# First mixture of a perceiver block: three dense tiles and five tiles by expert blocks, changed to eight tiles by expert blocks in two groups

## The chip, the cores and the metric

The kernel runs on one core of one Trainium2 chip. The metric is the device time of one launch in microseconds. All data are float32.

## The reference, cut to what matters

x is 16 x 64 x 256 (1024 tokens of width 256), the context is 16 x 1601 x 256. Six residual stages follow each other, each on the normalised x:

```
x = x + deformable_attention(ctx, ctx, norm(x))   # 16 heads, 5 sampled keys per query and head
x = x + sigmoid_attention(norm(x))                # inside a batch of 64 tokens
x = x + mixture0(norm(x))                         # 8 experts, hidden width 512, top 2
x = x + cross_attention(norm(x), ctx)             # 16 heads of 64; 77 text and 1524 image keys
x = x + state_space(norm(x))                      # scan over 64 tokens
x = x + mixture1(norm(x))                         # 32 experts, hidden width 128, top 4

def mixture0(x):
    p = softmax(router(rms(x)));  w = top-2 of p, renormalised, times per_expert_scale
    y_e = (gelu(x @ gate_e.T) * (x @ up_e.T)) @ linear_e
    return sum_e w_e * y_e
```

A token needs only two of the eight experts. The choice is made by the data, so a kernel can either run all experts on all tokens of a tile and weight the results (dense), or sort tokens by expert into blocks of 128 rows and run one expert per block.

## The kernel before, in words

The 1024 tokens lie in `x4` as 8 tiles of 128 tokens (two batches of 64 each). Work on TensorE, VectorE and ScalarE is issued in the order in which the Python generators are advanced (`tc.manual_schedule`); SyncE (SP) issues weight and context loads, GpSimd (POOL) issues the indirect DMAs, each engine in its own program order.

*Keys and values.* `keys_values` runs in 113 steps: it turns pieces of the context (`cx` to `cxt`), multiplies them by `wkv` (TensorE, L381) and ScalarE copies the result to `kv` (L382), which goes to the tables `tab` in DRAM (L385). Beside it run `samples` (where each head looks), `texts` (until step 60) and, from step 60 on, what stands in the list `mids`.

*Gathers and attends.* There are 32 units (8 tiles by 4 groups of 4 heads). `gather` does half a unit: VectorE copies the indices (`ig`, L427), then POOL issues ten indirect DMAs (L429). `attend` is the VectorE and ScalarE work of a unit (L449 to L481), in two halves. Their place in the program is chosen by `tick`, a count of microseconds that is only an estimate made while the program is built: a gather no sooner than `APART` (16) after the one before, `APART_X` (12) from the cross-attention on; an attend no sooner than `AFTER` (42) after its gather was issued.

*Attention and first mixture (middle).* `attention` finishes the deformable attention of one or two tiles and does the sigmoid attention. `middle` does the router. For tiles 0 to 2 (`ND0 = 3`) it goes on to run all eight experts on the whole tile (dense), two tiles as one group and one tile alone, each expert as two gate loads and one linear load of 512 KB into the four buffers `w`. For tiles 3 to 7 it writes the normalised rows to `x0d` and the routing to a `Table`; `slots` sorts, and `gelus` runs 17 blocks of 128 rows: an indirect DMA fetches the rows (`xb`, L853), SP reads the expert's number and loads 1.5 MB of its weights into five buffers `w`, and the result goes to `y0d`. `combine` fetches each token's two results back (`yk`, L654) and adds them to x.

*Cross-attention.* `Cross.step` is called 131 times; each does one pair of heads of one batch. TensorE multiplies the folded query `qf` with the turned context (`st`, shown at L88, the helper `mm`), VectorE takes maxima (`mp`, L1090), the maximum is turned and spread (L1109, `mc` L1121), VectorE subtracts and ScalarE exponentiates (L1130, L1131), and TensorE multiplies by the context (L1059) one step later. `fold(n + 1)` (L1123) makes the query of the next pair. Two batches make a tile, so 16 steps use one tile of x; they can go no further than the tiles whose first mixture is done. A step takes up to four generators (`side`, `mid`, `more`, `late`), which it advances at four places.

*The order at the top.* Keys and values with the first tiles beside them; the rest of those tiles alone; cross steps 0 to 26 with the remaining gathers and attends; cross steps 27 to 41 with attention and first mixture of tiles 3 to 7, what is left of it being drained before step 42; cross steps 42 to 130 with the state space of three quarters of the tokens; then the second mixture.

```python
        side = chain([middle(ND0, 1, lp, mw, tb0)]
                     + [z for t0 in range(ND0 + 1, NPAIR, TG) for z in (attention(t0, TG, lp, mw), middle(t0, TG, lp, mw, tb0))]
                     + [tb0.slots, lambda: gelus(lp, tb0), lambda: combine(lp, tb0, ND0, y0d, lambda t: None, 1)])
        while side.gi_frame and cr.n < NHP * 2 * ND0 - 6:
            cr.step(side, side, side, side)
            next(side, None)
        drain(side)
```

Of the kernel before, what the change touches and what calls it, by code (L numbers as in the profile page):

```python
# [27 lines left out]
APART, APART_X, AFTER = 16.0, 12.0, 42.0  # L28
# [25 lines left out]
ND0 = 3  # L54
# [11 lines left out]
def perceiver_kernel(ctx: ExitStack, tc: tile.TileContext, a: dict, out: bass.AP):  # L66
# [369 lines left out]
    def attend(i):  # L436

        j, h0 = units[i]
        if j not in cvs:
            cvs[j] = mk(const, [P, D], "cv", bufs=NPAIR - ND0)  # L440
# [101 lines left out]

    NT0 = NPAIR - ND0
    x0d, y0d = mk(dram, [NT0 * P, D], "x0d"), mk(dram, [blocks_of(NT0, E0, TOP0) * P, D], "y0d")
# [125 lines left out]
    class Middle:  # L670

        def __init__(self, lp, tag=None):
            self.tag = "x" if tag else "z"

            def wload(name, n, src):
                return load(lp, tag or name, src, [P, KC, n], 5 if tag else 1)

            self.bs = biases(lp, "lbias", ("bo", "abqkv", "abo", "als", "pes"), a["bias_a"])
            qkv = a["awqkvT"].rearrange(kp, p=P)
            self.wo = wload("wo", D, a["woT"].rearrange(kp, p=P))  # L680
            self.wqkv = [wload("wqk", 2 * D, qkv[:, :, : 2 * D]), wload("wv", D, qkv[:, :, 2 * D :])]
            self.awo = wload("awo", D, a["awoT"].rearrange(kp, p=P))

    def attention(t0, nt, lp, mw):
# [16 lines left out]
        xn = normed(range(t0, t0 + nt), mw.tag, lp)  # L701
# [3 lines left out]
        xt = turned(xn, nt, mw.tag, lp)  # L705
# [50 lines left out]
    def middle(t0, nt, lp, mw, tb=None):  # L756


        tiles = range(t0, t0 + nt)
        tok = nt * P  # L760
        xg = x4[:, t0 : t0 + nt, :]

        def wload(src, shape):
            return load(lp, "w", src, shape, 4)

        xn = normed(tiles, "x", lp)
        if tb is not None:
            q0 = (t0 - ND0) * P
            nc.sync.dma_start(out=x0d[q0 : q0 + tok, :].rearrange("(t p) d -> p t d", p=P), in_=xn)
        yield  # L770


# [9 lines left out]
        cw = mk(lp, [P, nt, E0], "cw")  # L782
        for t in range(nt):
# [6 lines left out]
            c = cw[:, t, :]  # L790
            if tb is not None:
                j = tiles[t] - ND0
                c = tb.gate[:, j, :]
                nc.vector.tensor_copy(tb.mask[:, j, :], m)
                tb.number(j)
# [9 lines left out]
        if tb is not None:  # L805
            return
        nh = HID0 // 2
        held = None

        def second(e, act, lin):  # L810
            po = bank()[:, : nt * D].rearrange("p (t d) -> p t d", t=nt)
            for t in range(nt):
                mm(po[:, t, :], [(act[:, c, t * P : (t + 1) * P], lin[:, c, :]) for c in range(HID0 // P)])
                nc.vector.scalar_tensor_tensor(
                    xg[:, t, :], po[:, t, :], cw[:, t, e : e + 1], xg[:, t, :], ALU.mult, ALU.add
                )

        for e in range(E0):
            act = mk(lp, [P, HID0 // P, tok], "act")
            lin = None  # L820
            for hf in range(2):
                wg = wload(a["gate0"][e, hf].rearrange("(k p) i h -> p k i h", p=P), [P, KC, 2, nh])
                if hf:
                    lin = wload(a["lin0"][e].rearrange("(c p) d -> p c d", p=P), [P, HID0 // P, D])
                for c in range(nh // P):
                    ph = bank()[:, : 2 * tok].rearrange("p (i n) -> p i n", i=2)
                    for i in range(2):
                        mm(ph[:, i, :], [(wg[:, k, i, c * P : (c + 1) * P], xt[:, k, :]) for k in range(KC)])
                    if held and hf * 2 + c == 1:
                        second(*held)  # L830
                        held = None
                    gl = mk(lp, [P, tok], "gl")
                    nc.scalar.activation(gl, ph[:, 0, :], AF.Gelu_apprx_tanh)
                    nc.vector.tensor_tensor(act[:, hf * 2 + c, :], gl, ph[:, 1, :], ALU.mult)
                    yield
            held = (e, act, lin)
        second(*held)
        yield

    def gelus(lp, tb):  # L840
# [4 lines left out]
        def fetch(i):  # L845
            if i >= tb.nb:
                return
            if i % 4 == 0:
# [5 lines left out]
                out=x, out_offset=None, in_=x0d, in_offset=bass.IndirectOffsetOnAxis(ap=tb.row[:, i : i + 1], axis=0)  # L854
# [3 lines left out]
            for hf in range(2):  # L858
                w.append(load(lp, "w", a["gate0"][bass.ds(v, 1), hf].rearrange("o (k p) i h -> p (o k) i h", p=P), [P, KC, 2, nh], 5))
            w.append(load(lp, "w", a["lin0"][bass.ds(v, 1)].rearrange("o (c p) d -> p (o c) d", p=P), [P, HID0 // P, D], 5))  # L860
# [10 lines left out]
        def second(i, act, lin):  # L871
            po = bank()
            mm(po[:, :D], [(act[:, c, :], lin[:, c, :]) for c in range(HID0 // P)])
            y = mk(lp, [P, D], "y")
            nc.scalar.copy(y, po[:, :D])
            nc.scalar.dma_start(out=y0d[i * P : (i + 1) * P, :], in_=y)
# [30 lines left out]
    class Cross:  # L907
# [98 lines left out]
        def fold(self, n):  # L1006
# [10 lines left out]
            qf = self.qf[n] = mk(self.xp, [P, KC, P], "qf", bufs=2)  # L1017
# [52 lines left out]
        def step(self, side=None, mid=None, more=None, late=None):  # L1070
# [52 lines left out]
            self.fold(n + 1)  # L1123
# [43 lines left out]
        def begin(self, xp):  # L1167
# [16 lines left out]
            self.fold(0)  # L1184
            yield
# [6 lines left out]
    class Ssm:  # L1192
# [15 lines left out]
        def group(self, g, wide=None):  # L1208
# [67 lines left out]
            dx = mk(mp, sh, "dx")  # L1276
# [466 lines left out]
```

## Time and profile before

| what | value |
|---|---|
| median of 3 runs | 3313.22 us (3308.72 to 3315.46) |
| the profiled execution | 3307.06 us, its span 3305.1 us |
| busy: TensorE, VectorE, ScalarE, GpSimd | 2924.7, 1620.0, 1026.4, 818.2 us |
| granted TensorE clock, mean | 0.946 |
| moved by DMA | 326.06 MB, 99 GB/s over the span |

The span is read by stages, since the limits differ:

| stage | us from the span's start |
|---|---|
| keys and values, with two tiles' attention and 5 of 8 dense experts beside them | 0 to 711 |
| the remaining dense work, alone | 711 to 885 |
| the cross-attention's start | 885 to 912 |
| cross steps 0 to 26, with gathers and attends | 912 to 1402 |
| cross steps 27 to 41, with attention and mixture of tiles 3 to 7, and the drain | 1402 to 1811 |
| cross steps 42 to 130, with the state space | 1811 to 3005 |
| second mixture | 3005 to 3305 |

Busy times of TensorE are of matmul records, whose ends are modelled. Every float32 matmul leaves two records.

### The profile page before, as it was taken

The page shows a single profiled execution, that of the slowest core. Times are in us where ns is not written, and L with a number is a line of the kernel's source. Part 1 is how long each engine was busy: PE and PEld are TensorE (multiplying, and loading weights), DVE is VectorE, ACT ScalarE, POOL GpSimd, SP SyncE. Part 2 cuts the span into 40 slices and gives each one's busy share as a digit, 9 for nine tenths or more (in the row PEclk, how much of TensorE's full clock was granted, in tenths as well). Part 3 has the DMA queues.
Part 4 walks back from the last instruction along what each step waited for, and adds up shares of the span by engine and source line. Part 5 has one row for each costly group of instructions (what it writes and reads, how often), then busy time and mean ns, then how long its engine had stood idle before and what let it go on. Part 6 is the DMA issues. An engine that isn't in the chain of part 4 may idle for free.

```text
span 3305.1 us, 46546 instructions
## 1 busy us (share of the span) xinstructions
PE 2924.7 (88%) x17734; PEld 2402.8 (73%) x17734; DVE 1620.0 (49%) x4143; ACT 1026.4 (31%) x2379; POOL 818.2 (25%) x923
## 2 busy tenths in 40 slices
PE   8779887995678888987997999999999999998879
PEld 4444444564567777876897999989999999896667
DVE  2421113224345445655332577557654487655846
ACT  3233333323212211233242433334323333222421
POOL 0444335545455455200001011001100011000721
PEclk9889998997789899988998999999999999999999
DMA  6387754662511211200454121112210122003884
GB/s 203 102 148 159 239 155 128 180 194 83 154 24 30 58 52 38 75 23 30 137 175 148 44 62 59 50 45 71 66 34 30 57 66 63 26 1 115 257 239 123
DMA packets 339015, 326.06 MB, mean 99 GB/s; under 512 B 59349, under 2 KB 289017, under 8 KB 338281
## 3 DMA queue, kind: packets, MB, share of 16 engines
q1 hardware_dynamic: 186297, 225.11, 22.9%
q10 hardware_dynamic: 126928, 63.06, 7.0%
q0 software_dynamic: 25568, 34.91, 4.9%
q8 instruction: 141, 2.31, 0.3%
q14 instruction: 81, 0.66, 0.1%
HBM read 248.37 MB, written 74.62 MB: 98 GB/s over the span
## 4 chain that ended last, share of the span: by engine, by line
PE 74%; DVE 10%; another core or an unknown queue 5%; issue 4%; DMA 3%; ACT 3%; POOL 0%; SPq 0%; DVEq 0%; ACTq 0%; POOLq 0%
PE st L88 31%; PE mm L1059 19%; PE mm L88 15%; PE mm L153 5%; PE mm L1015 2%; DMA wg<-in_guT 1%; PE mm L1045 1%; DVE hs L1298 1%; DVE mp L1090 1%; PE mm L984 1%; DVE pt L1130 1%; DMA w<-in_gate 1%; PE mm L1109 1%; DVE hc L1303 0%
## 5 line engine op out<-in xcount | busy, mean ns | idle before, releaser
L88 PE MATMUL st<-qf,cT 128*128 128x128 f32 x6144 | 761.3, 282 | 42.2 <-ACT qf L1018 31.9
L429 POOL DMA_INDIRECT g<-tab,ig x640 | 616.2, 963 | 720.8 <-DVE ig L427 519.6
L88 PEld LDWEIGHTS st<-qf,cT 128*128 128x128 f32 x6144 | 739.8, 198 | 52.4 <-ACT qf L1018 35.6
L1059 PE MATMUL mm<-cn,pt 128*128 128x257 f32 (+1 forms) x3072 | 755.8, 390 | 2.0 <-DVE cT L84 1.2
L1059 PEld LDWEIGHTS mm<-cn,pt 128*128 128x128 f32 (+1 forms) x3072 | 563.8, 193 | 88.0 <-DVE cT L84 2.0
L88 PE MATMUL st<-wkv,cxt 128*128 128x512 f32 (+1 forms) x832 | 401.4, 629 | 53.7 <-ACT kv L382 28.7
L1090 DVE TENSOR_REDUCE mp<-st 128x128 f32<-128x512 f32 x384 | 261.1, 688 | 253.5 <-PE st L88 232.6
L88 PEld LDWEIGHTS st<-wkv,cxt 128*128 128x128 f32 (+1 forms) x832 | 157.0, 198 | 226.8 <-issue 178.1
L1130 DVE TENSOR_TENSOR pt<-st,mc 128x512 f32<-128x512 f32 (+1 forms) x384 | 224.2, 640 | 156.5 <-ACT mc L1121 133.9
L1131 ACT ACTIVATE pt<-pt 128x512 f32<-128x512 f32 (+1 forms) x384 | 207.3, 588 | 57.6 <-DVE pt L1130 51.2
L382 ACT COPY kv<-st 128x512 f32<-128x512 f32 (+1 forms) x208 | 118.9, 591 | 234.1 <-PE st L88 128.7
L1121 ACT COPY mc<-mm 128x128 f32<-128x128 f32 x128 | 33.9, 265 | 464.8 <-PE mm L1119 328.4
L1111 DVE TENSOR_REDUCE xmx<-mm 128x1 f32<-128x128 f32 x128 | 37.3, 292 | 229.3 <-PE mm L1109 180.1
L1068 ACT COPY ot<-mm 128x256 f32<-128x256 f32 x128 | 47.2, 369 | 294.8 <-PE mm L153 294.7
L920 POOL MEMSET cn<- 128x12 f32 x16 | 1.8, 119 | 544.5 <-PE mm L1059 520.3
L461 DVE TENSOR_REDUCE smx<-sc 128x4 f32<-128x20 f32 x32 | 5.4, 168 | 244.5 <-ACT sc L459 233.9
L1304 POOL TENSOR_TENSOR ys<-ys,hc 128x512 f32<-128x512 f32 x64 | 81.5, 1273 | 161.2 <-DVE hc L1303 160.9
L1388 POOL DMA_INDIRECT xb<-xnd,row x55 | 55.2, 1004 | 262.9 <-PE mm L1045 221.6
L88 PE MATMUL mm<-xt,w 128*128 128x256 f32 (+1 forms) x512 | 103.0, 359 | 14.3 <-issue 8.4
L88 PEld LDWEIGHTS mm<-xt,w 128*128 128x128 f32 x512 | 89.6, 218 | 31.0 <-issue 21.2
L1035 ACT COPY yt<-mm 128x64 f32<-128x64 f32 x128 | 27.2, 212 | 252.7 <-PE mm L88 230.6
L153 PEld LDWEIGHTS mm<-ident,cx 128*128 128x128 f32 (+1 forms) x416 | 54.9, 150 | 44.4 <-issue 31.7
(455 smaller groups left out, 3994.5 us busy)
## 6 DMA issues: line engine op xcount, KB each, us to landing
tab<-kv ACTq DMA_DIRECT2D x48, 1024.0 KB
w<-in_gate SPq DMA_DIRECT2D x66, 512.0 KB
cx<-in_ctx SPq DMA_DIRECT2D x48, 512.0 KB
cn<-in_ctx SPq DMA_DIRECT2D x16, 1408.0 KB
wg<-in_guT SPq DMA_DIRECT2D x87, 256.0 KB
w<-in_lin SPq DMA_DIRECT2D x33, 512.0 KB
wk<-in_xwkiT SPq DMA_DIRECT2D x32, 512.0 KB
wd<-in_down1T SPq DMA_DIRECT2D x87, 128.0 KB
```

The lines of the kernel that those rows point to most:

```text
L88: nc.tensor.matmul(o, lhsT=l, rhs=r, start=i == 0, stop=i == len(pairs) - 1)
L153: nc.tensor.transpose(t[:ncol, i, :rows], b, ident[:rows, :rows])
L382: nc.scalar.copy(kv[:w, :, c, :], pk[:w].rearrange("p (h e) -> p h e", h=H0))
L429: nc.gpsimd.indirect_dma_start(out=gf[:, (half * n + s) * 4 * HD0 : (half * n + s + 1) * 4 * HD0], out_offset=None, in_=tables[j], in_offs ...
L1015: nc.tensor.matmul(pf[:, k * P : (k + 1) * P], lhsT=w[:, hp % 4, k * P : (k + 1) * P], rhs=rhs, start=True, stop=True)
L1059: nc.tensor.matmul(po, lhsT=pt[:w, c, :], rhs=cn[:w, c, :], start=c == 0, stop=c == NCH - 1)
L1068: nc.scalar.copy(ot, tp[:, :KC, :])
L1090: nc.vector.tensor_reduce(mp_[:, i, :], s.rearrange("p c n -> p n c"), AX.X, ALU.max)
L1130: nc.vector.tensor_tensor(o, st[i][:, :m, :], mc.to_broadcast([P, m, P]), ALU.subtract)
L1131: nc.scalar.activation(o, o, AF.Exp)
L1304: nc.gpsimd.tensor_tensor(y, y, hc, ALU.add)
L1388: nc.gpsimd.indirect_dma_start(out=x, out_offset=None, in_=xnd, in_offset=bass.IndirectOffsetOnAxis(ap=tb.row[:, i : i + 1], axis=0))
```

## The change: what it does

All eight tiles take the way of blocks, in two groups of four tiles (`first(0)`, `first(1)`), 15 blocks each; the dense part is gone. The first group stands in `mids` beside keys and values, where `mid` is now called twice in a step; the second is the `side` of cross steps. Both use five buffers `w`, which also hold the attention's weights. The first group has tiles 2 and 3 attended singly, so that each can begin when its own units are done. `APART` is 12 everywhere. `fold` runs two pairs of heads ahead, with three buffers `qf`. In the state space `dx` and `ys` take the buffers of the tags `mt` and `mn`. `more` is given to every second step alone.

```diff
-APART, APART_X, AFTER = 16.0, 12.0, 42.0
+APART, AFTER = 12.0, 42.0
...
-ND0 = 3
+WB0 = 5
...
-            cvs[j] = mk(const, [P, D], "cv", bufs=NPAIR - ND0)
+            cvs[j] = mk(const, [P, D], "cv", bufs=4)
...
-    NT0 = NPAIR - ND0
-    x0d, y0d = mk(dram, [NT0 * P, D], "x0d"), mk(dram, [blocks_of(NT0, E0, TOP0) * P, D], "y0d")
+    NT0 = NPAIR // 2
+    x0d = [mk(dram, [NT0 * P, D], f"x0d{i}") for i in range(2)]
+    y0d = [mk(dram, [blocks_of(NT0, E0, TOP0) * P, D], f"y0d{i}") for i in range(2)]
...
-        if tb is not None:
-            return
-        nh = HID0 // 2
-        held = None
...
-        for e in range(E0):
-            act = mk(lp, [P, HID0 // P, tok], "act")
...
-        second(*held)
-        yield
-
-    def gelus(lp, tb):
+
+    def gelus(lp, tb, half):
...
-            qf = self.qf[n] = mk(self.xp, [P, KC, P], "qf", bufs=2)
+            qf = self.qf[n] = mk(self.xp, [P, KC, P], "qf", bufs=3)
...
-            self.fold(n + 1)
+            self.fold(n + 2)
...
             self.fold(0)
+            self.fold(1)
...
-            dx = mk(mp, sh, "dx")
-            y = mk(mp, sh, "ys")
+            dx = mk(mp, sh, "mt")
+            y = mk(mp, sh, "mn")
...
-            pace["gather"] = now + (APART if cr is None else APART_X)
+            pace["gather"] = now + APART
...
+        def first(half):
+
+            tb, mw, t0 = Table(lp, NT0, E0, TOP0), Middle(lp), half * NT0
+            return [
+                (4 * (t0 + 2), attention(t0, TG, lp, mw)), (0, middle(t0, TG, lp, mw, tb)),
+                (4 * (t0 + 3), attention(t0 + 2, 1, lp, mw)), (4 * (t0 + 4), attention(t0 + 3, 1, lp, mw)),
+                (0, middle(t0 + 2, TG, lp, mw, tb)), (0, tb.slots()), (0, gelus(lp, tb, half)),
+                (0, combine(lp, tb, t0, y0d[half], lambda t: None, 1)),
+            ]
...
-                mw = Middle(lp)
-                for t0, nt in ((0, TG), (TG, ND0 - TG)):
-                    mids += [(4 * (t0 + nt), attention(t0, nt, lp, mw)), (0, middle(t0, nt, lp, mw))]
-                late = attention(ND0, 1, lp, mw)
+                mids = first(0)
...
             if lp:
+                mid()
                 mid()
...
-        side = chain([middle(ND0, 1, lp, mw, tb0)]
...
-        while side.gi_frame and cr.n < NHP * 2 * ND0 - 6:
-            cr.step(side, side, side, side)
-            next(side, None)
+        side = chain([z for _, z in first(1)])
+        while side.gi_frame and cr.n < NHP * 2 * NT0 - 6:
+            cr.step(side, side, side if cr.n % 2 else None, side)
         drain(side)
```

## The prediction

> **What bounds the kernel now.** I read three things in this order: the page for the engines, the busy times by stage, then single rows of the timeline where a stage loses time. The page says that TensorE carries the end, and that POOL has one large group, the gathers.
>
> ```profile
> PE 2924.7 (88%) x17734; PEld 2402.8 (73%) x17734; DVE 1620.0 (49%) x4143; ACT 1026.4 (31%) x2379; POOL 818.2 (25%) x923
> L429 POOL DMA_INDIRECT g<-tab,ig x640 | 616.2, 963 | 720.8 <-DVE ig L427 519.6
> ```
>
> By stage (columns: window, length, busy PE, PEld, DVE, ACT, POOL, granted clock, DMA share, GB/s):
>
> ```profile
> 578.00:711.00 133.00, 127.02 (x457) 80.07 (x456) 36.24 (x111) 51.32 (x94) 71.00 (x74) 0.99 0.62 175
> 711.00:885.00 174.00, 116.24 (x535) 95.89 (x533) 68.99 (x219) 46.68 (x93) 90.04 (x96) 0.79 0.45 130
> 912.00:1402.00 490.00, 400.28 (x2696) 357.65 (x2696) 255.23 (x647) 98.82 (x269) 234.00 (x248) 0.92 0.18 46
> 1402.00:1625.00 223.00, 183.34 (x1170) 163.22 (x1171) 114.36 (x383) 71.14 (x163) 3.92 (x5) 0.90 0.17 52
> 1625.00:1763.00 138.00, 136.62 (x1032) 127.93 (x1031) 44.53 (x102) 53.90 (x114) 12.40 (x14) 1.00 0.58 183
> 1763.00:1811.00 48.00, 31.57 (x226) 28.48 (x224) 12.32 (x29) 9.87 (x22) 10.40 (x16) 0.89 0.34 103
> 1811.00:3005.00 1194.00, 1185.52 (x8787) 1087.96 (x8788) 744.78 (x1671) 408.46 (x995) 67.80 (x108) 1.00 0.16 47
> ```
>
> From 1811 to 3005 TensorE is full at clock 1.00; nothing of the change touches that stage but the place of one fold. The losses lie ahead of it: dense work alone at clock 0.79 (711 to 885), cross steps with gathers (912 to 1402), attention beside cross steps (1402 to 1625), a drain (1763 to 1811). Only from 1625 to 1763, blocks beside cross steps, is TensorE full there too. Single rows of the timeline:
>
> ```profile
> 1041.32 0.94 POOL L429 DMA_INDIRECT g<-tab,ig  x1 [0.30 <-issue]
> 1042.57 0.94 POOL L429 DMA_INDIRECT g<-tab,ig  x1 [0.30 <-issue]
> 1073.38 5.40 PE L88 MATMUL st<-qf,cT 128*128 128x128 f32 x32 [4.00 <-ACT qf L1018]
> 1789.97 0.94 POOL L654 DMA_INDIRECT yk<-y0d,sli  x1 [29.82 <-DMA y0d<-y]
> 1811.35 0.48 PE L1109 MATMUL mm<-ident,mp 128*128 128x128 f32 x1 [16.27 <-DVE mp L1092]
> ```
>
> One indirect DMA holds POOL 1.25 us from start to start, so a gather of ten holds it 12.5 us. A folded query can come late by 4 us. The draining `combine` leaves TensorE 16 us without work.
>
> **The change part by part.** Which step does what I take from the order of instructions in the two programs.
>
> *Work of TensorE.* A block is 16 products of 128 columns, 4 of 256 and two turns: from the rows `mm<-ct,w` (1.95 us for half of the 16), `mm<-w,bact` (1.89) and `ident,xb` (0.38), less their overlap, 5.7 us. A dense expert on two tiles takes 10.7 us (7.07 + 3.9 at 718), on one tile about 5.4. Before: 8 x 10.7 + 8 x 5.4 + 17 x 5.7 = 226 us; after: 30 x 5.7 = 171. So 55 us of work go; the stages decide where. Weights fall from 24 MB + 25.5 MB to 45 MB.
>
> *Stage 1, keys and values (711 us before).* Before, it holds the attention of two tiles and 5.25 experts; after, the attention and router of four tiles, `slots` and 5.5 blocks, and 46 gathers in place of 30, 42 attend halves in place of 28. Work of TensorE changes by -56 + 31 + 16 = -9 us, but chains replace products. A tile's attention and router alone took 27.5 us (752.5 to 780), 13.8 of it idle; `mid` now runs twice in a row, so that half the hand-overs have no projection between them. By pieces: attention +30, `slots` +12, blocks +31 and +24 for their first rows and weights and for rows that wait for gathers, 7 more units of attend at some 3 us each +21, dense work -32 (20 steps at 6.45 us, 578 to 707, against 4.85 for steps without it), which is +86. The lower end is POOL's: from step 60 (399 us) to the end there are 26 gathers and 8 row fetches, 26 x 12.5 + 8 x 1.25 = 335 us where the stage had 312, thus +23 at least unless POOL falls behind. I take **+79**, near the sum by pieces, because this trace shows such chains always dear.
>
> [...] The row: clock 0.99 while dense products fill the stage, 0.79 where chains stand alone. [...] If the whole tail of stage 1 (250 us of work) fell to 0.79 it would cost 66 us; by the row of 399 to 578 (attention beside keys and values, clock 0.90 to 0.94), about 20, which is inside my +79.
>
> *Stage 2, alone (174 us before).* After: 9.5 blocks. With weights in hand a block took 6.25 us (1774.9 to 1781.2); 1.5 MB at the 281 GB/s seen at 3100 to 3200 take 5.3, and five buffers hold less than two blocks, so I take 8: 76 us. Rows: a fetch issued behind a gather waits 12.5 + 1.25 us and lands 2.8 us after its start (1789.97 to VectorE at 1792.73), 16.5 against a lead of one to one and a half blocks; three gathers fall here, 5 us each, 15. Then `combine`: eight jobs at 1.74 us (1792.73 to 1808.35 for nine), 3 us for the last store and one gather in front, 30. Together 121: **-53**. Between 95 (all hidden) and 150 (12 us a block, as the lone dense tile took).
>
> [...] No run here shows a row fetch behind a gather: before, all gathers ended at 1352 and the first `xb` came at 1597. [...]
>
> *Stage 3, cross steps with gathers.* Before, gathers 40 to 63 stand in the cross steps, after 50 to 63. 23 steps from 921.4 to 1346.8 give 18.5 us a step; a clean step is 12.3 and one with the turn of the context 15.8, 12.8 on average. Ten steps fewer with a gather: 10 x 5.7 = **-57**. The cover is that these steps' own chain of VectorE and ScalarE is freed of attends; if the price of a gather were DMA and not VectorE, it would come back in stage 1.
>
> *Stage 4, attention and blocks beside cross steps.* Before 409 us for 15 steps, 217 over the bare 192. Attention of five tiles and `slots` cost 223 - 9 x 12.8 = 108; four tiles with 3.5 generators a step in place of 5 save **-13**. Two blocks fewer: **-11**. The drain: its step took 48 us, less 15.8 for a step with a turn and 8 for the last blocks, 24; after, `combine` ends by step 41, sixteen steps ahead of its limit, and its eight jobs cost VectorE some 0.9 us each in the steps: **-17**. Step 42 follows in both programs, and the state space starts there in both.
>
> *Fold.* The waits of `st` for `qf` are 31.9 us of TensorE, all of them between 912 and 1390. With the query ready one group of `st` (1.8 us) can start; the next needs the buffer that VectorE's subtraction frees, which is late next. Seven such waits remain in the shorter stage: **-12**, between 0 and -30. `mt` and `mn`, `cv` with four buffers, SP's loads: nothing, since what they wait for is earlier in the program by a whole generator; a context load behind a weight load that waits for its buffer has two pieces (four steps, 25 us) of lead. Should that lead go, stage 1 pays what is left, at most some 10 us.
>
> Sum: 79 - 53 - 57 - 41 - 12 = -84 against the profiled 3307.06, so 3223; the median of the runs is 6 us above that execution: **3229**.
>
> **The rivals.**
>
> *POOL's queue becomes the bound (slower).* Place: blocks 0 to 14 of the first group, in stages 1 and 2. For it: 12.5 us of every 13 to 14 are POOL's once gathers stand 12 apart beside blocks. Against it: the tick counts about what the stage takes, so POOL keeps pace. [...]
>
> *Half clock in stage 1.* The tail at 0.79, 66 in place of 20: 3275. For it the row 711:885, against it that projections still come between.
>
> *Better cover.* Stage 1 ends at POOL's floor, +23, and stage 2 at 95: 3147. For it the idle time that stage 1 had before (108 us from 0 to 711), against it that TensorE keeps program order.
>
> *The change doesn't do what it says*: if the second group weren't done in time, a drain would stand at step 58. The order shows it done by step 41, so I give that 0.01.
>
> **How the numbers follow.** A measurement of this kernel can tell about 0.2%, 7 us, from no change. Forecast 0.52, half clock 0.20, better cover 0.10, POOL 0.17, the last 0.01. All of the better case, nearly all of the forecast and most of half clock (whose ends pass 3307 when stage 2 is dear too) are faster: 0.78; 0.05 within 0.2%; 0.17 slower. The range 3150 to 3325 takes in half clock and the forecast with nearly all its ends; it leaves out the upper half of the POOL case and part of the better one.
>
> **What would show it.** Right: keys and values end near 790, cross steps start near 940, step 42 comes near 1725, the stage after it keeps 1194 us, waits for `qf` fall under 15 us, and no 16 us gap stands before step 42. Wrong: `xb` rows at the head of long TensorE waits, clock under 0.85 from 400 to 800, cross steps with gathers faster or slower than 18.5 us, or a longer stage after step 42.

## The result, and the profile after

The changed kernel takes 3350.84 us (median of 9 runs, 3342.42 to 3359.04), the kernel before 3313.56 us on the same chip (3308.72 to 3338.99): a ratio of 1.0096, with a 95% interval of 1.0074 to 1.0119. It is 37 us slower. The forecast was 3229 us, and its range went from 3150 to 3325.

The page of the changed kernel (busy time, share of the span, instructions; the group of gathers):

```profile
PE 2859.0 (85%) x17594; PEld 2344.7 (70%) x17594; DVE 1612.3 (48%) x4141; ACT 1024.5 (31%) x2367; POOL 832.4 (25%) x947
L429 POOL DMA_INDIRECT g<-tab,ig x640 | 611.0, 955 | 650.6 <-DVE ig L427 429.8
```

TensorE has 66 us less to do, where 55 were forecast, and the span is 44 us longer: idle time grew by 110 us. The stages of the changed kernel (window, length, busy PE, PEld, DVE, ACT, POOL, granted clock, DMA share, GB/s; at 444 us `keys_values` is in the middle, where `mids` begins):

```profile
0.00:444.00 444.00, 335.84 (x1016) 177.42 (x1017) 120.39 (x399) 125.06 (x250) 196.52 (x224) 0.88 0.61 151
444.00:735.00 291.00, 195.81 (x556) 100.67 (x555) 79.56 (x261) 85.74 (x167) 143.14 (x151) 0.80 0.42 116
735.00:912.00 177.00, 100.63 (x398) 65.01 (x397) 50.98 (x200) 41.40 (x84) 98.31 (x103) 0.77 0.44 127
912.00:1080.00 168.00, 85.80 (x536) 78.33 (x535) 39.95 (x107) 33.55 (x72) 67.59 (x73) 0.76 0.55 169
1089.00:1341.00 252.00, 201.03 (x1351) 179.35 (x1352) 126.30 (x325) 51.01 (x136) 131.78 (x138) 0.93 0.16 40
1341.00:1859.00 518.00, 497.97 (x3632) 453.83 (x3631) 256.00 (x695) 195.17 (x428) 24.12 (x38) 0.99 0.30 93
1859.00:3049.00 1190.00, 1181.90 (x8783) 1085.12 (x8782) 743.93 (x1670) 407.20 (x992) 67.88 (x108) 1.00 0.15 47
```

The kernel before reaches the same point of `keys_values` 45 us sooner, with as much work done on TensorE:

```profile
0.00:399.00 399.00, 329.72 (x1017) 174.44 (x1018) 105.05 (x355) 126.74 (x250) 142.51 (x160) 0.92 0.69 168
```

From cross step 0 on, the change does what it should: 1341 to 1859, attention and blocks beside cross steps, is nearly full (498 of 518 us) at clock 0.99, and the stage after step 42 is as long as before. All of the loss stands ahead of the first cross step, in the first four lines; 45 us of it come before the blocks and the new chains begin. Single rows there (start, length; in brackets the idle time before and what ended it):

```profile
850.73 3.79 PE L88 MATMUL mm<-ct,w 128*128 128x128 f32 x16 [16.42 <-ACT ct L819]
...
1024.06 0.94 POOL L429 DMA_INDIRECT g<-tab,ig  x1 [0.30 <-issue]
1025.31 0.95 POOL L655 DMA_INDIRECT yk<-y0d,sli  x1 [0.30 <-issue]
...
1032.32 0.94 POOL L655 DMA_INDIRECT yk<-y0d,sli  x1 [1.22 <-DVE ig L427]
1033.57 0.94 POOL L429 DMA_INDIRECT g<-tab,ig  x1 [0.30 <-DVE x L666]
...
1044.80 0.94 POOL L429 DMA_INDIRECT g<-tab,ig  x1 [0.30 <-issue]
1046.05 0.95 POOL L655 DMA_INDIRECT yk<-y0d,sli  x1 [0.30 <-issue]
...
1055.16 0.66 PE L153 MATMUL mm<-ident,qn 128*128 128x128 f32 x2 [35.67 <-DVE qn L103]
1858.59 0.27 PE L1060 MATMUL mm<-ident,mp 128*128 128x128 f32 x1
```

At 850.73 a product of an early block waits 16.42 us. The eight fetches of `combine` (`yk`) stand behind one gather of ten and around another, and TensorE has nothing for 35.67 us. The 16 us hole before step 42 (1811.35 in the kernel before) is gone: the last row has no idle time in front.

The experiments are read by the same points in every kernel's profiled run, in us from the span's start (a step's time is that of the turn of its `mp`). Most of them ran on other chips, and those fall into two kinds: on the first, the kernel before takes 3297 to 3319 us, as in this result; on the second 3061 to 3069. So each total is compared with the kernel before on its own chip; the rows of one kind come from different chips, whose medians differ by up to 22 us.

| kernel | kind | keys and values end | first cross product | step 0 | step 14 | step 42 | step 127 | end |
|---|---|---|---|---|---|---|---|---|
| before | first | 707 | 912 | 921 | 1179 | 1811 | 2994 | 3305 |
| changed | first | 912 | 1080 | 1089 | 1341 | 1859 | 3038 | 3350 |
| e1, changed, gathers 16 apart | first | 694 | 1053 | 1060 | 1300 | 1823 | 3019 | 3330 |
| e2, before, gathers 12 apart | first | 871 | 1031 | 1040 | 1309 | 1865 | 3038 | 3349 |
| e4, changed, no gathers | first | 668 | 796 | 804 | 989 | 1507 | 2687 | 2998 |
| h2, changed, pause | first | 888 | 1010 | 1017 | 1270 | 1768 | 2994 | 3307 |
| h3, changed, five of ten | first | 676 | 821 | 830 | 1025 | 1542 | 2721 | 3034 |
| e5, before, no gathers | second | 609 | 783 | 791 | 975 | 1559 | 2742 | 3055 |
| e8, before with the fold | second | 615 | 791 | 800 | 985 | 1570 | 2749 | 3060 |
| f1, changed | second | 696 | 854 | 862 | 1050 | 1568 | 2748 | 3059 |
| f2, changed, pause | second | 693 | 816 | 824 | 1007 | 1476 | 2702 | 3010 |

### The profile page after: what moved, and what is told of

Its sections match the earlier page's. It is cut to its first block, busy times and chain, and to the rows that moved or that the text cites. A ratio compares the mean times of both kernels' runs of the same rounds, so it can differ in the third digit from the quotient of the medians.

```text
span 3349.5 us, 46546 instructions
## 1 busy us (share of the span) xinstructions
PE 2859.0 (85%) x17594; PEld 2344.7 (70%) x17594; DVE 1612.3 (48%) x4141; ACT 1024.5 (31%) x2367; POOL 832.4 (25%) x947
## 4 chain that ended last, share of the span: by engine, by line
PE 54%; DVE 7%; DMA 2%; ACT 2%; issue 2%; another core or an unknown queue 1%; SPq 0%; POOL 0%; DVEq 0%; ACTq 0%; POOLq 0%
PE st L88 20%; PE mm L1010 19%; PE mm L88 8%; PE mm L153 3%; PE mm L966 2%; DMA wg<-in_guT 1%; PE mm L996 1%; DVE hs L1250 1%; DVE mp L1041 1%; PE mm L935 1%; DVE pt L1081 1%; ACT pt L1082 1%; PE mm L1060 1%; DVE hc L1255 0%
## 5 line engine op out<-in xcount | busy, mean ns | idle before, releaser
L88 PE MATMUL st<-qf,cT 128*128 128x128 f32 x6144 | 744.0, 277 | 17.8 <-issue 16.5
L1010 PE MATMUL mm<-cn,pt 128*128 128x257 f32 (+1 forms) x3072 | 747.8, 387 | 2.3 <-issue 2.0
L88 PEld LDWEIGHTS st<-qf,cT 128*128 128x128 f32 x6144 | 722.5, 194 | 24.3 <-issue 20.1
L88 PE MATMUL st<-wkv,cxt 128*128 128x512 f32 (+1 forms) x832 | 408.6, 638 | 51.3 <-ACT kv L382 42.3
L88 PE MATMUL mm<-ct,w 128*128 128x128 f32 x960 | 132.0, 295 | 59.5 <-ACT ct L819 50.8
L88 PEld LDWEIGHTS mm<-ct,w 128*128 128x128 f32 x960 | 125.7, 209 | 68.4 <-ACT ct L819 54.8
L849 DVE TENSOR_TENSOR bact<-gl,mm 128x256 f32<-128x256 f32 x60 | 25.3, 421 | 249.0 <-ACT gl L848 223.0
L1256 POOL TENSOR_TENSOR mn<-mn,hc 128x512 f32<-128x512 f32 x64 | 81.6, 1275 | 161.1 <-DVE hc L1255 157.0
```

Source lines behind the costliest of these rows:

```text
L88: nc.tensor.matmul(o, lhsT=l, rhs=r, start=i == 0, stop=i == len(pairs) - 1)
L1010: nc.tensor.matmul(po, lhsT=pt[:w, c, :], rhs=cn[:w, c, :], start=c == 0, stop=c == NCH - 1)
L1256: nc.gpsimd.tensor_tensor(y, y, hc, ALU.add)
```

## The experiments

My theory after the result: a gather costs the other engines time where it stands, more so where gathers stand close, and the change moved ten of them ahead of the cross steps and all of them closer. The rivals: the attends' VectorE work; the chains of four tiles with `mid` twice in a step; row fetches behind gathers in POOL's queue.

### Spacing and what a gather's price is (e1 to e4, first kind)

**e1**: the changed kernel with the old spacing.

```diff
-APART, AFTER = 12.0, 42.0
+APART, APART_X, AFTER = 16.0, 12.0, 42.0
-            pace["gather"] = now + APART
+            pace["gather"] = now + (APART if cr is None else APART_X)
```

> The changed kernel with gathers 16 apart until the cross-attention, as before the change. Theory G (closer gathers are what keys and values can't bear: step 60 came at 444 us in place of 399 with six gathers more): step 60 returns to about 400, the stage of keys and values ends near 740 in place of 905, all 15 blocks then stand alone (about 110 us), some six more steps keep gathers (+35 us), total near 3270. Theory C (chains: attention, sorting and blocks beside keys and values, with mid called twice, are what is dear): step 60 returns, but from there to the first cross step the time stays near 645 us, total 3320 or more.

Measured: 3329.54 us against 3298.15 for the kernel before, 1.0105 (1.0079 to 1.0132). Keys and values end at 694 in place of 912, and the stage after it takes 359 us in place of 168. PE's waits of that stage (in all, times, longest):

```profile
PE mm L153 <- DVE vb L477: 49.8, 1, 49.8
PE mm L153 <- DVE qn L103: 41.5, 1, 41.5
PE mm L88 <- ACT ct L819: 26.7, 11, 9.9
```

`vb` is the end of an attend: tile 3 waits for units whose gathers come late. Four tiles ahead of the cross steps need 32 half units, and the old spacing had 29 of the 64 out when keys and values ended. The loss only changes its place. By its total this is also what the rival of the chains had (3320 or more); e4 decides against that rival, since it has the same chains and reaches the first cross product at 796.

**e2**: the kernel before with `APART` 12 everywhere, nothing else.

> The kernel before with gathers 12 apart from the start, that part alone. Theory G: step 60 at about 445, the stage of keys and values longer by 100 us or more, cross steps with gathers shorter by 40 to 60 us, total 3340 to 3380. Theory C: step 60 at 440 but no more is lost later, the cross steps give 50 us back, total within 10 us of 3313.

Measured: 3345.11 us, 1.0150 (1.0122 to 1.0177). Closer gathers alone lengthen keys and values from 707 to 871. Part of that is dense work that moved in (169 of TensorE's products, from the stage alone, which falls from 205 to 160), so the first cross product comes 119 us later; the cross steps up to step 42 get back 65 us (890 to 825).

**e3**: the changed kernel without the attends' arithmetic (two small additions on the gathered rows stay).

> The changed kernel; an attend is left out but for two small additions of VectorE that read the gathered rows (no scores, no exponential). Theory G, in the form that POOL's time and the DMAs cost: step 60 stays at 435 to 445. In the form that VectorE's and ScalarE's work of attends costs: step 60 at 405 or less. The whole falls by some 100 us in any case, since the cross steps lose their attends too; the stage of cross steps with gathers tells the price of an attend there: 13 us a step in place of 17.5 if it is the attends, 17 if it is the gathers.

Measured (one run): 3411.24 us, slower than the changed kernel, where about 100 us less were expected. Nearly all of it is lost in keys and values between 199 and 391 us, where the same products take the changed kernel 131; there, a hundred indirect DMAs follow each other without a pause (207 to 332), where the changed kernel's longest row is of thirty. One run can't say whether that is the reason, and so e3 gives no price of an attend in that stage. **e4**: the ten indirect DMAs of a gather give way to one memset; attends stay.

```diff
-        for s in range(n):
-            nc.gpsimd.indirect_dma_start(
-                out=gf[...
+        nc.gpsimd.memset(gf[:, half * n * 4 * HD0 : (half + 1) * n * 4 * HD0], 0.01)
```

> The changed kernel; the ten indirect DMAs of each half unit are left out and give way to one memset on POOL, all attends stay. Theory G in the form of POOL and DMAs: step 60 at 400 or less, no TensorE wait for rows of x over 5 us in the first group, keys and values end below 760, cross steps near 13 to 14 us. In the form of attends: step 60 at 430 or more and cross steps at 17.

Measured (one run): 2999.44 us. Cross steps 0 to 13 of e4, and then of e3, to be read beside the line 1089 to 1341 above:

```profile
804.00:989.00 185.00, 179.47 (x1347) 164.96 (x1348) 125.46 (x322) 52.19 (x136) 6.15 (x11) 1.00 0.10 30
```

```profile
1156.00:1403.00 247.00, 201.49 (x1350) 178.70 (x1351) 87.58 (x217) 50.15 (x129) 129.40 (x138) 0.92 0.15 41
```

With the attends' full VectorE work (125.46 us) and no gathers, 14 steps take 185 us; with gathers and a third less VectorE work, 247. So nearly all of the price of a step with a gather is the gather. The theory that blamed VectorE falls. In the whole kernel the gathers cost 3351 - 2999, some 351 us (on two chips of the first kind, so to some 20 us).

### Is the loss in the gathers or in the rest? (e5 to e8, second kind)

**e5**: the kernel before with the memset of e4.

> The kernel before with the ten indirect DMAs of each gather replaced by one GpSimd memset (the gathered data are left out, attends stay). The changed kernel without gathers took 2999 us, its first cross step at 804 us. If gathers are what eats the forecast gain (a gather costs more where more of them stand close), the kernel before without them keeps the forecast difference: about 3080 us, first cross step near 780. If the blocks, the chains of the fourth tile and mid called twice cost what the forecast did not see, it stands well below: about 2960 us, first cross step near 640, since the changed kernel lost 168 us there.

Measured: 3056.38 us (one run), and on this chip the kernel before takes 3069.42: its gathers cost 13 us here, where they cost about 250 on the first kind. Without gathers the changed kernel (e4, 2999) is 57 us faster than the kernel before, of the 84 that the sum had. That comparison crosses the kinds, but outside the gathers the kinds can't be told apart: in every trace here the third batch's first product of keys and values comes at 82 to 85 us, before the first gather starts at 94 to 96, and from step 64 to the end all take 1181 to 1187 us.

**e6** and **e7**: the changed kernel with half of the gathered bytes, in ten DMAs of half width and in five of full width.

```diff
-                out=gf[:, (half * n + s) * 4 * HD0 : (half * n + s + 1) * 4 * HD0],
+                out=gf[:, (half * n + s) * 4 * HD0 : (half * n + s) * 4 * HD0 + 2 * HD0],
```

```diff
-        for s in range(n):
+        for s in range(n // 2):
```

> The changed kernel with ten indirect DMAs a gather as before, each of half the bytes (the other half of the gathered data is set to a constant by VectorE). If a gather's price is that of its descriptors on GpSimd's queue, it stays at some 3350 us (first cross step 1089 us, 12.5 us a gather on GpSimd). If it is the bytes that pass the DMA engines, about half of the 351 us that gathers cost is gone: some 3175 us.

> The changed kernel with five indirect DMAs a gather in place of ten, each of full width (the rest of the gathered data is set to a constant by VectorE). Same bytes as the run with ten of half width. If the price is descriptors and their time on GpSimd, half or more of the 351 us goes: 3175 us or less, first cross step near 930; less still if it is gathers standing in a row, since five take 6.3 us of every 12. If it were bytes, it gives the same time as the run with ten of half width.

Measured (one run each): 3057.77 and 3013.15 us. The expectations were reckoned for the first kind, so the totals can't decide as written there; beside the changed kernel on the second kind (f1, 3057.00) they do: half the bytes change nothing, half the DMAs save 44 us, most of the 58 that gathers cost the changed kernel there (3057 against 2999 without them). On the first kind bytes alone were not tried.

**e8**: the kernel before with the fold two pairs ahead.

```diff
...
-            self.fold(n + 1)
+            self.fold(n + 2)
...
```

> The kernel before with one part of the change: queries folded two head pairs ahead, three buffers qf, and dx and ys in the buffers of mt and mn. The forecast put this part at -12 us (0 to -30) in the changed kernel; here, where the waits for qf are 31.9 us between 912 and 1390 us, -10 to -25 us, ratio 0.993 to 0.997. If the wait only moves to the buffer that VectorE's subtraction frees, no difference: 0.999 to 1.001.

Measured: 0.9992 (0.9985 to 0.9999), 2.7 us, in place of the 10 to 25 expected. There is little to save on this kind: with the old fold, e5 waits 0.9 us for `qf` in its cross steps 0 to 26. On the first kind the fold alone was not tried. There the changed kernel has no wait for `qf` left (31.9 us before), but in the steps with gathers waits for `mp` rose from 15.3 to 22.0 us:

```profile
PE mm L1060 <- DVE mp L1043: 22.0, 4, 11.8
PE st L88 <- issue: 16.5, 22, 1.7
```

### The queue of POOL (f1 to f3 second kind, h1 to h3 first)

**f1** is the changed kernel as it is.

> The changed kernel as it is, beside the kernel before, on the chip of these runs. The kernel before took 3313 and 3298 us on two chips and 3069 us on a third, where leaving out its gathers saved only 13 us. If the loss comes from what gathers do on the slow pair of chips, the changed kernel is faster than before wherever the kernel before takes some 3070 us: about 3015 to 3060 us, ratio 0.98 to 0.997. Where it takes some 3300 us, the ratio stays at 1.010. If the loss is in the blocks and chains themselves, the ratio is above 1.005 on either chip.

Measured: 3057.00 us, 0.9974 (0.9964 to 0.9985). On the second kind the change makes the kernel faster, by 7 us, just short of the 0.98 to 0.997 expected. A loss in the blocks and chains themselves would have shown here too.

**f2**: no gather is issued from the first group's first block to the end of its `combine`.

```diff
-        if pace["open"] and now >= pace["gather"] and ...
+        if pace["open"] and not pace["hold"] and now >= pace["gather"] and ...
...
+        def held(gen, free):
+            pace["hold"] = True
+            yield from gen
+            pace["hold"] = not free
...
-                ... (0, gelus(lp, tb, half)),
-                (0, combine(lp, tb, t0, y0d[half], lambda t: None, 1)),
+                ... (0, held(gelus(lp, tb, half), False)),
+                (0, held(combine(lp, tb, t0, y0d[half], lambda t: None, 1), True)),
```

> The changed kernel with no gather issued from the first group's first block to the end of its combine, so that no row fetch stands behind a gather on GpSimd's queue. If rows behind gathers are what the first group pays (the rival POOL's queue; 83 us of such waits and the 36 us hole at combine stand in the changed kernel's trace), stage 2 falls by 50 to 100 us and the whole is 0.97 to 0.99 of the changed kernel. If a gather costs 5 to 6 us wherever it stands, those that are put off cost the same in cross steps: within 0.5% of the changed kernel.

Measured: 3010.67 us, 0.983 (0.981 to 0.985) of the kernel before and 46 us under f1. The dense stage between keys and values and the cross steps, first f1 and then f2:

```profile
696.00:854.00 158.00, 86.66 (x535) 77.80 (x534) 39.88 (x107) 33.19 (x72) 67.83 (x72) 0.77 0.58 182
```

```profile
693.00:816.00 123.00, 78.65 (x534) 71.01 (x533) 26.91 (x68) 27.59 (x65) 15.28 (x18) 0.85 0.67 218
```

The same 534 products in 123 us in place of 158. The waits of TensorE at the end of `combine`, in f1 and in f2:

```profile
829.29 0.66 PE L153 MATMUL mm<-ident,qn 128*128 128x128 f32 x2 [35.65 <-DVE qn L103]
```

```profile
791.38 0.66 PE L153 MATMUL mm<-ident,qn 128*128 128x128 f32 x2 [20.22 <-DVE qn L103]
```

That is 15 of the 35 us. Another 9.5 are waits for rows of `xb` that no longer stand behind a gather, and 8 are TensorE's busy time itself, with the granted clock at 0.85 in place of 0.77.

**f3**: groups of 3 and 5 tiles.

> The changed kernel with groups of 3 and 5 tiles in place of 4 and 4 (13 and 17 blocks), the second with the five generators a step of the kernel before, to be done before step 42. If what the changed kernel lost is the price of gathers that must be in before the cross steps start (32 half units there against 24 here), the cross steps start 60 to 120 us sooner than in the changed kernel and the end comes 20 to 60 us sooner: 0.982 to 0.994 of the changed kernel. If a gather's price is the same in cross steps, the gain of the start is given back: within 0.5%.

Measured: 3040.25 us, 0.9923 (0.9906 to 0.9941), which is 0.9945 of f1 by the medians. Step 0 comes at 790 in place of 862, but step 42 at 1550 in place of 1568: three quarters of the gain are given back. The larger second group stands in fewer cross steps, which may be why; it was not tried apart. The result falls between what the two theories expected.

**h2** is f2 again, on the first kind.

> The kernel of the run that paused gathers in the first group's blocks and combine, once more, for the chip of these runs. Where the kernel before takes about 3065 us, 0.983 again. Where it takes about 3300: rows behind gathers and the hole at combine cost at least as much there (83 and 36 us of waits), so 0.985 to 0.997 if they are the loss; 1.000 to 1.010 if put-off gathers cost the same 5 to 6 us in cross steps.

Measured: 3310.03 us against 3318.61, 0.9979 (0.9958 to 1.0000). It falls between the two expectations. Against the changed kernel's 1.0096 the pause saves 1.2%, some 39 us (the two ratios come from different chips, so this is known to some 10 us), much as on the second kind, and its middle stage is the same again:

```profile
888.00:1010.00 122.00, 79.27 (x535) 71.40 (x534) 27.09 (x68) 27.89 (x66) 15.32 (x18) 0.86 0.68 220
```

So POOL's queue is one part of the loss on both kinds. It is not what separates them: keys and values still end at 888. In f2 and h2 the second group's `combine` ends at step 49, not 41 as without the pause, so their step 42 in the table comes too early for the work done; counted at step 64, f2 is 46 us ahead of f1 and h2 44 ahead of the changed kernel.

**h1** starts the pause at `slots` and gives `side` to all four places of a cross step.

> The changed kernel with no gather issued from the first group's slots to the end of its combine, and with side given to all four places of every cross step of the second group. Where the kernel before takes about 3065 us: the first block's rows no longer stand behind a gather (15.6 us in the run that paused from the first block on), and less of the second group is left to be drained before step 58: 2985 to 3005 us, ratio 0.974 to 0.981. Where it takes about 3300: if a gather costs 5.7 us wherever it stands, 1.000 to 1.005; if standing beside blocks made it dear, 0.985 to 0.995.

Measured on the first kind: 1.0019 (0.9997 to 1.0042), no better than h2 and rather worse.

**h3** is e7 again, on the first kind.

> The changed kernel with five indirect DMAs a gather in place of ten (the rest of the gathered data is set to a constant), once more, for the chip of these runs. Where the kernel before takes about 3065 us, 3013 us again. Where it takes about 3300: if the price goes with the number of indirect DMAs, half of the 351 us is left, 3175 us; if it comes only where gathers follow each other without a pause, 3020 to 3080 us, since five take 6.3 us of every 12.

Measured (one run): 3035.76 us, as expected if the price comes where gathers follow each other without a pause. Half the DMAs take away 315 of the 351 us. Five DMAs in the time of ten are nearly free; the second five cost nearly everything. But h3 has half the DMAs, half the bytes and shorter rows (at most ten without a pause, against twenty and thirty in the changed kernel's keys and values) at once.

### Fives (k1, k2, m1 second kind, n1 first)

Is it the row of ten without a pause, or their number in a stretch of time? **k1** is f2 with each gather cut into two fives, 7.8 us of the program's count apart; **k2** is the kernel before with the same.

```diff
-        i, half = divmod(k, 2)
+        i, half = divmod(k, 4)
-        n = HU * NK // 2
+        n = HU * NK // 4
-            pace["gather"] = now + APART
+            pace["gather"] = max(pace["gather"] + APART, now)
```

> The changed kernel with gathers paused in the first group's blocks and combine, and every gather of ten indirect DMAs cut into two of five, a five no sooner than 7.8 us of the program's count after the one before. Same number of DMAs. Where the kernel before takes about 3315 us: if rows of ten without a pause are what is dear, 3040 to 3150 us (0.92 to 0.95 of before); if it is the number of DMAs in a stretch of time, some 3300 (0.99 to 1.00). Where before takes about 3065 us, where gathers cost little: 3000 to 3025 us (0.979 to 0.987) in both.

> The kernel before with gathers cut into fives in the same way, 7.8 us apart (ten in 15.6 us as before in stage 1, and in cross steps where it was 12). Where before takes about 3315 us: 3090 to 3200 (0.93 to 0.97) if rows of ten are dear, 3280 to 3330 (0.99 to 1.005) if the number in a stretch of time is. Where before takes about 3065: 0.995 to 1.005.

Both fell on the second kind, where they can't tell: k1 0.9831 (0.9814 to 0.9847), k2 1.0002 (0.9992 to 1.0012). k1 once more, again on the second kind:

> The kernel with gathers in fives and paused in the first group's blocks and combine, once more, for the chip of this run. Where the kernel before takes about 3315 us, the same kernel with tens took 0.9979 of it: 0.92 to 0.96 if rows of ten without a pause are dear, 0.985 to 1.005 if the number of DMAs in a stretch of time is. Where before takes about 3065 us, 0.983 again.

Measured: 0.9806 (0.9785 to 0.9826). **n1**, h1 in fives:

> The changed kernel with no gather from the first group's slots to the end of its combine, side at all four places of a cross step, and gathers in fives 7.8 us apart. Where the kernel before takes about 3065 us: 2985 to 3005 us (0.974 to 0.981) if the 15.6 us wait of the first block's rows goes; 0.981 to 0.984 if it is only exchanged for another. Where before takes about 3315 us, the same kernel with tens took 1.0019 of it: 0.92 to 0.96 if rows of ten without a pause are dear, 0.99 to 1.005 if the number of DMAs is.

It fell on the first kind: 3347.54 us, 1.0152 (1.0101 to 1.0204), where h1 with tens took 1.0019; neither expectation had that much. So fives in the program are no cure. But they don't answer the question, since hardly a five stands by itself in the trace of keys and values: POOL waits for VectorE's index copies and then runs twenty indirect DMAs without a pause (301.57 to 326, 341.06 to 366, 380.98 to 406), as in the changed kernel. The end of one row and the start of the next in n1:

```profile
325.35 0.94 POOL L429 DMA_INDIRECT g<-tab,ig  x1 [0.30 <-issue]
341.06 0.94 POOL L429 DMA_INDIRECT g<-tab,ig  x1 [14.77 <-DVE ig L427]
```

Whether the price goes with the length of a row or with the number of DMAs in a stretch of time stays open.

## Why the prediction was wrong, by its own steps

On the first kind the four differences are +205 (keys and values), -37 (the stage alone, to the first cross product), -120 (cross steps up to 42) and about -3 after it; +45 in the profiled spans. The sum had +79, -53, -110 and 0.

**Stage 1, "I take +79": the step that failed.** It came out at +205 on the first kind and at +81 on the second (696 in f1, 615 in e8). The pieces for attention, `slots`, blocks and dense work were thus sized well in sum; what they lacked is the gathers. I priced sixteen more of them by POOL's own time alone ("+23 at least") and by the attends' VectorE work, and otherwise put what they cost the other engines at nothing. What a gather costs the other engines in keys and values, from the runs without gathers (609 us for the structure of before, 668 for the changed one):

| kernel | kind | gathers of ten begun before the end of keys and values | us each |
|---|---|---|---|
| before | first | 30 | (707 - 609) / 30 = 3.3 |
| before, 12 apart (e2) | first | 46 | (871 - 609) / 46 = 5.7 |
| changed | first | 45 | (912 - 668) / 45 = 5.4 |
| changed, five of ten (h3) | first | 23 (45 of five) | (676 - 668) / 23 = 0.3 |
| changed (f1) | second | 45 | (696 - 668) / 45 = 0.6 |

Fifteen more at 3.3 would be 50 us; that all 45 went from 3.3 to 5.4 is another 95. Together 145, the difference of 205 from the 59 of the structure alone. e2 shows it without any of the rest of the change: its +164 come from `APART` alone. The e2 row is somewhat too high, for the dense work that moved in. Counted to the first cross product, where each structure has done the same work on TensorE, a gather costs (912 - 783) / 40 = 3.2 in the kernel before, (1031 - 783) / 54 = 4.6 in e2 and (1080 - 796) / 50 = 5.7 in the changed kernel; e1, at the old spacing, has (1053 - 796) / 45 = 5.7 too, with the waits for its late units in it.

**Stage 3, -57: the amount came, its reason didn't.** Up to step 42 the first kind saved 120 us and the second 64; the 56 between them go with the ten gathers that left the cross steps. (The first kind's number has the fold in it, the second's, taken from e8, has not; so the match is in part luck.) And the price was the gather and not the attends beside it (e3, e4). The text said that in this case it would come back in stage 1, and the sum gave that no weight. It came back more than doubled. On the second kind there was little to save: 14 steps with gathers take 188 us, 13.4 each.

**Stage 2, -53.** To the first cross product it came out at -37 and, on the second kind, at -18 (176 to 158). The prediction's 121 us reach to the query's turn (`qn`). Up to there the stage took 143 us in the changed kernel and 133 in f1, and with the pause 98 in f2 and in h2. The sum without its waits for gathers (15 for rows, 12.5 for the one gather in front of `combine`) is 93. So the 8 us a block and the eight jobs of `combine` were about right; the waits, with the lower clock beside them, came to 45 and 35 us in place of 27.5, with two gathers among the fetches of `combine` and not one. The rest of the shortfall on the second kind is that the same stage of the kernel before takes 29 us less there. That is the rival of POOL's queue, in its place. No run had shown a row fetch behind a gather when the sum was made, so the 27.5 us of such waits in it, like those within the 24 of stage 1, were the author's estimate, and so was the rival's price: up to 8.5 us for each of 15 blocks (12.5 for a gather, 1.25 for the fetch and 2.8 until its rows are used, less 8 for a block), 100 us more than the sum had. The runs show less than half of that: the pause saves 39 us of the whole on the first kind and 46 on the second. The waiting itself stands in the rows at 1024 to 1046: POOL starts a fetch at 1032.32, the ten of a gather from 1033.57 to 1044.80, 1.25 us apart, and the next fetch at 1046.05.

**Half clock.** The clock in stage 1 is indeed lower, 0.80 and 0.77 after 444 us: a mean of stretches such as 238 to 257 us, where it is 0.50, and 258 to 281, where it is 1.00. What brings it down was not tried. The same instructions of keys and values are busy for 632 us in the changed kernel, at a mean clock of 0.83, and for 591 in f1 on the second kind, at 0.92: 41 us. Keys and values end 216 us apart. So the longer busy time has 41 of these us, and the rest is idle time.

**Stage 4, fold, the rest.** -120 against -110 up to step 42: the total is right on the first kind, and the 16 us hole is gone, but the terms can't be told apart there. The fold's waits for `qf` went as said (31.9 us to none), and waits for `mp` rose by 7 us. After step 42 nothing changed.

## What to carry to other kernels

A price seen beside a piece of work (here 5.7 us a step with a gather) moves with it: before taking it as a gain, name what causes it by a run that leaves out one candidate, and charge it to the place where the work goes. Indirect DMAs share POOL's queue with the small fetches behind them (a fetch behind a gather of ten starts 12.5 us after the gather's first); keeping them out of the short stretch where other engines wait for such a fetch saved 39 to 46 us here. With it the changed kernel is 0.983 of the kernel before on one kind of chip; on the other, at 0.9979 (0.9958 to 1.0000), it is at least no slower.

## What the runs showed of the hardware that was not expected

Two kinds of chips: the kernel before takes 3313.56, 3298.15, 3318.61 and 3296.99 us in four sets of runs and 3069.42, 3064.41, 3067.43 and 3061.10 in four others, and without gathers about 3056. The same change is 1.0096 on the one and 0.9974 on the other. An indirect DMA holds POOL as long on both (963 ns in the kernel before, 964 in e8). The packets of POOL's queue take 82 ns each in the kernel before and 85 in the changed one on the first kind, 87 in e8 and 78 in f1 on the second (60 to 700 us; the queue's 7.4, 8.9, 9.3 and 11.1% of 16 engines' time over its 9280, 10785, 10901 and 14608 packets). What differs is when other engines go on. ScalarE's waits from 100 to 600 us in the kernel before, and then in f1 on the second kind:

```profile
ACT kv L382 <- PE st L88: 81.7, 67, 5.1
ACT kv L382 <- remote: 45.1, 11, 7.8
ACT kv L382 <- issue: 32.5, 20, 5.7
ACT cxt L398 <- remote: 17.1, 3, 11.3
```

```profile
ACT kv L382 <- PE st L88: 139.1, 134, 2.3
...
ACT kv L382 <- DMA tab<-kv: 12.5, 5, 4.0
```

Single copies of the changed kernel on the first kind, beside a row of thirty indirect DMAs (210 to 247):

```profile
225.59 0.42 ACT L521 COPY kts<-mm 128x308 f32<-128x308 f32 x1 [3.13 <-PE st L88]
233.35 0.59 ACT L398 COPY cxt<-mm 128x512 f32<-128x512 f32 x1 [7.34 <-PE st L88]
242.46 0.59 ACT L382 COPY kv<-st 128x512 f32<-128x512 f32 x1 [8.52 <-issue]
250.85 0.59 ACT L382 COPY kv<-st 128x512 f32<-128x512 f32 x1 [7.81 <-remote]
```

One copy in 8 us, with waits that end on TensorE, on nothing that the profile shows ("issue") or on a releaser that it doesn't know ("remote"). None of the longest of ScalarE's waits is "remote" in f1, e4, e5 or h3. So on the first kind, dense indirect DMAs delay what other engines wait for (351 us of the changed kernel, where the second kind has 58), though their packets take as long on the second. Half the number, with half the bytes and in shorter rows, takes nearly all of it away (h3); half the bytes alone changed nothing where that was tried (e6, second kind). Which of these counts on the first kind, which path is delayed, and what makes the two kinds of chips, no run shows.
